# A gated feed-forward layer with quantised activations: the place of a sum, the fillers' budget, a bank's first write and the order of the tail

## The chip, the cores and the metric

The kernel runs on one core of a Trainium2 chip. The metric is the device time of one execution in microseconds (us), the median of three runs. TensorE is called PE here, VectorE DVE, ScalarE ACT, GpSimd POOL; SP is the engine that issues nearly all DMAs, in one queue that is taken strictly in order. Each engine also takes its own instructions in order: an instruction that waits holds up all that stand behind it on its engine.

## The reference

The input is x with four batches of 1024 tokens of 512 numbers, all in float32. For every batch the layer computes

```python
scale = cond @ norm_w.T + 1.0
h = x * (scale[:, None, :] * rsqrt(mean(x * x) + EPS))
u = h @ up_w.T                        # 512 -> 2 x 2048
val, gate = split(u, 2)
h = val * gelu(gate)                  # 2048 per token
hq = act_quant(h)                     # per token: round(h * 127/max|h|), and back
y = hq @ weight_quant(down_w).T + x   # weights -1, 0, 1 times a mean
```

(hq and the quantised weights are written there with a stop_gradient, which changes no value.) The maximum over a token's 2048 values has to be known before any of them can be rounded.

## The kernel before, in words

A batch has two halves of 512 tokens, and a half four tiles of 128 (a = 0 to 3). The 2048 hidden rows are 16 blocks j. For batch 1 and later the kernel works in *slots*, one for each block: `slot` (L581 on) issues the seven fast-multiplication products of the up projection of block g = 16 b + j (A, E, B banks of PSUM; each product is six 128x512 matmuls, L513). The products 3, 2 of the block before it are finished in the same slot. ACT applies the Gelu (L608, L624), DVE multiplies and writes the hidden values into H, a ring of 18 slots (L611, L630). In a slot there are places for other work: `early` at its start, `x`, `mid[0]`, `y`, `mid[1]`, `mid[2]`, `late`, `z`.

Batch b - 1 is quantised and multiplied by the down weights while batch b goes through its slots. DVE scales a piece of two blocks and one half (`quant_scale`, L705); it is rounded by one DVE instruction (`quant_round`, L709) or by two of ACT (`quant_up`, `quant_down`, L713, L717). The down product of token tile a of both halves is one `Pair`, done in slot j = 10 + a of batches 1 and 2 (`DOWN`), also as a fast multiplication, with sums instead of an eighth product. Its steps are:

- `sum1` (L760): the pair's first sum, on DVE, written into the H place of the next block, which is not yet in use as such. In slot 11 that place is still the source of a DMA transpose of token tile 0 of the next batch (L499).
- `sums` (L767 to L769): three more sums on DVE.
- `first`: B11 into bank k1, an ACT copy (L792), T1 into k3, which takes the first sum as its weights, B21 onto k1.
- `third`: T2, an ACT copy (L801), and DVE adds k3 to the rows of x (`onto`, L824).
- `fourth`: B22, T3, an ACT copy (L810), DVE L824 for k1.
- `fifth`: T4 onto k2, which needs that copy, DVE L824 for k2, and the two stores (L819).

The three banks k1, k2, k3 rotate through the PSUM tag "po". Before the first pair of all, `late` writes each of the three once with a matmul named po_set (L1307).

`next_pair` makes the pair of the next slot and issues its `sum1`. In the slot before the first pair it runs in `mid[0]` behind the weight sums (`d_sums`, L417: 2 x 1.2 us on DVE each); in the others in `early`, behind the running pair's `sums`.

The next batch's tokens are prepared in the same slots: ACT squares (L447), DVE L421 and POOL L422 make the factor, ACT (L459) and POOL (L460) scale, POOL adds (L468 to L471), ACT and DVE split into high and low parts (L492, L496), and SP's transpose brings them into place.

DVE's other work comes from a list, the `Filler`: maxima over pairs of blocks (L647, L649) and the pieces. At `x` and `z` of each slot it takes from the list what a budget allows: `left` is a slot's length less what is known to be in it, `cap` the part for `x`. The order on each engine is thus fixed when the program is made.

In the tail batch 3 has no slots after it. Pair 3 of batch 2 is done as plain products there (`down_mm`, L733, for both halves, and `down_end`, L742), next to pair 2 in the fast form (`old[2]`). Then come the two halves of batch 3: `half_steps` gives the scaling and rounding of their eight pieces, `token_turn` (L682) and `token_undo` (L688) send the maxima through DRAM and bring them back as a factor for each token (dq_end), which DVE inverts and scales (`bring_dq`, L691, L692). `down_end` multiplies by it, adds x and stores (L743).

```python
def early():
    if down:
        pair.first([po_bank(f"po_{b}_{a}_{n}") for n in range(3)])
        pair.sums()
        next_pair()
    d_sums(early_sums)
```

Of the kernel before, what the change touches and what calls it, by code (L numbers as in the profile page):

```python
# [18 lines left out]
P = 128  # L19
# [31 lines left out]
def glu_quant_kernel(  # L51
# [11 lines left out]
    B, S, D = x.shape  # L63
# [6 lines left out]
    NJ = FF // P  # L70
# [80 lines left out]
    def po_bank(name, shape=None):  # L151
        return bank("po", 3, shape, name)
# [1050 lines left out]
    for b in range(1, B):  # L1203
        dve, act = Filler(), Filler()
        gains(b)
        am = am_tile(b - 1)
        dq = state[b - 1] = sm.tile([P, 2 * NA], F32, name=f"dq_{b}", tag="dq")
        last_pair = NJ // 2 - 1
        for h in range(2):
            add_pair(  # L1210
                dve, act, b - 1, last_pair, h, (0, "xz"[h]),
                lambda now, h=h: token_max(b - 1, h, am),
            )
        for h in range(2):
            for cost, f in token_scale(h, am):
                dve.add((1, "x"), cost, lambda now, f=f: f())
        add_pieces(dve, act, b - 1, am, PIECES, (2, "x"))
        for i in range(NJ // 2 - 1):
            for h in range(2):
                add_pair(dve, act, b, i, h, (2 * i + 3, "x"))  # L1220
        steps = {}
        pairs = {}
        if b + 1 < B:
            sc = cond_load_scale(b + 1)
            bring = lambda b=b, sc=sc: cond_bring(b + 1, sc)
            steps[1, "z"] = [(bring, (0.4, 0))]
            p0 = b * NJ + 12
            plan = [
                (None, p0, ((6, "z"), (7, "x"), (7, "y"), (9, "y"), (10, "x"), (10, "z"))),
                (p0 + 4, None, ((9, "y"), (10, "x"), (10, "y"), (11, "y"), (12, "x"), (12, "x"))),  # L1230
                (None, None, ((10, "y"), (11, "x"), (11, "y"), (13, "x"), (13, "y"), (13, "z"))),
                (p0 + 2, p0 + 4, ((9, "z"), (12, "x"), (12, "y"), (14, "x"), (14, "y"), (14, "z"))),
            ]
            for a, (at, nx_at, places) in enumerate(plan):
                def make(a=a, at=at, nx_at=nx_at, b=b):
                    toks[a] = Tokens(b + 1, a, at, nx_at)
                    toks[a].load()
                fs = [
                    make,
                    lambda a=a: toks[a].norm(),  # L1240
                    lambda a=a, sc=sc: toks[a].scale(sc),
                    lambda a=a: toks[a].high(),
                    lambda a=a: toks[a].low(DVE),
                    lambda a=a: toks[a].turn(),
                ]
                costs = ((0, 0), (0, 1.6), (0, 1.5), (0, 2.1), (2.6, 0), (0, 0))
                for place, f, c in zip(places, fs, costs):
                    steps.setdefault(place, []).append((f, c))
        for j in range(NJ):
            g = b * NJ + j  # L1250
            down = b + 1 < B and j in DOWN
            if down:
                pair, a = pairs[j], DOWN[j]
                xrs = [down_load(b - 1, h, a) for h in range(2)]
            early_sums, late_sums = D_SUM_AT.get((b, j), ((), ()))
            left = SLOT_US + PAIR_US * down - OWN_US + 0.4
            left -= D_SUM_US * (len(early_sums) + len(late_sums))
            mine = {p: [sum(c[e] for _, c in steps.get((j, p), ())) for e in range(2)] for p in "xyz"}
            left -= sum(mine[p][0] for p in "xyz")
            act_left = {"x": 2.7, "y": 2.2 if down else 1.1, "z": 0}  # L1260

            def run(p):
                nonlocal left
                for f, _ in steps.get((j, p), ()):
                    f()
                if p == "x":
                    cap = min(left, 3.9 - mine["x"][0] - (0 if down else mine["y"][0]))
                    left -= cap - dve.run((j, p), cap)
                elif p == "z":
                    left = dve.run((j, p), left)  # L1270
                if p != "z":
                    act.run((j, p), act_left[p] - mine[p][1])

            def early():
                if down:
                    pair.first([po_bank(f"po_{b}_{a}_{n}") for n in range(3)])
                    pair.sums()
                    next_pair()
                d_sums(early_sums)

            def next_pair():
                if b + 1 < B and j + 1 in DOWN:
                    pairs[j + 1] = Pair(b - 1, DOWN[j + 1])
                    pairs[j + 1].sum1(h_slots(g + 1)[:, 0, 0])

            def more_sums():
                d_sums(late_sums)
                next_pair()

            mid = [nothing] * 3  # L1290
            if j + 1 == min(DOWN):
                mid[0] = more_sums
            if down:
                mid = [lambda: (pair.third(xrs, dq), d_sums(late_sums)), pair.fourth, lambda: (loads(), pair.fifth())]

            def loads():
                if NJ + 2 <= g + 2 < B * NJ:
                    s_load_x(g + 2)
                if NJ + 2 <= g + 1 < B * NJ:
                    s_load_y(g + 1)  # L1300


            def late():
                if b == 1 and j + 1 == min(DOWN):

                    for n in range(3):
                        PE.matmul(  # L1307
                            po_bank(f"po_set_{n}").rearrange("p (a t) -> p a t", t=P),
                            s_tile(g + 1)[:, 0, 0, :P], t_view(b)[:, :, 0, 0, 0, :],
                            start=True, stop=True,  # L1310
                        )

            if b + 1 == B and j in DOWN and DOWN[j] < 3:
                pairs[DOWN[j]] = Pair(b - 1, DOWN[j])
                places = old_places(DOWN[j])
                pairs[DOWN[j]].sum1(places[0])
                pairs[DOWN[j]].sums(*places[1:])
            if j == 4:
                token_turn(b - 1, am)
            if j == 5:  # L1320
                bring_dq = token_undo(b - 1, dq)
            if j == 6:
                bring_dq()
            if j == NJ - 1:
                get_ready()
            elif b == 1 and j == 0:
                get_ready()
            slot(g, lambda: run("x"), lambda: run("y"), lambda: run("z"), early, mid, late)
            if not down:
                loads()  # L1330
        assert not act.items and not dve.items, (b, dve.items, act.items)
# [59 lines left out]
    def half_steps(h):  # L1391
        for i in range(NJ // 2):
            yield lambda i=i: quant_scale(b, i, h, am)
            if i % 3 == 2:
                yield lambda i=i: quant_round(b, i, h)
            else:
                def rounds(i=i):
                    quant_up(b, i, h)
                    quant_down(b, i, h)
                yield rounds  # L1400
# [24 lines left out]
    for f in work[2:7]:  # L1425
        f()
    down_mm(b - 1, 0, 3, pos[0], range(NJ // 2, NJ))
    down_mm(b - 1, 1, 3, pos[1], range(NJ))
    old[2].fifth()
    for f in work[7:11]:  # L1430
        f()
    for h in range(2):
# [2 lines left out]
        f()  # L1435
    work = [f for _, f in token_scale(1, am)] + [lambda: token_turn(b, am, 1, 2)]
    work += list(half_steps(1))
    for h in range(2):
        bring_dq = token_undo(b, dq, h, h + 1)
        if h == 0:  # L1440
            pos = [po_bank(f"po_end_0_{a}") for a in range(3)] + [bank("E", 2, name="po_end_0_3")]
        else:
            pos = [bank(t, 1 if t == "B" else 2, name=f"po_end_1_{n}") for n, t in enumerate("ABEA")]

        ys = [2] * (NA - 1) + [1 if h else 2]
        cut = NJ - 4
        for j in range(0, cut, 2):
            for a in range(NA):
                down_mm(b, h, a, pos[a][:, : HALF * ys[a]], (j, j + 1), 0, ys[a])
            for f in work[:4]:  # L1450
                f()
            del work[:4]
        for f in work:
            f()
        work = []
        bring_dq()
        for a in range(NA):
            c, xr = slice(0, HALF * ys[a]), XR[:, h * NA + a]
            down_mm(b, h, a, pos[a][:, c], range(cut, NJ), 0, ys[a])
            down_end(b, h, a, pos[a][:, c], xr[:, c], dq, c)  # L1460
# [30 lines left out]
```

## Time and profile before

| what | value |
|---|---|
| median of three runs | 749.37 us (748.68 to 750.09) |
| the profiled execution | 749.7 us, span 747.5 us |
| granted TensorE clock, mean | 0.997 |
| busy: DVE, ACT, POOL | 80%, 52%, 28% of the span |
| DMA, mean | 148 GB/s |
| chain that ended last, largest parts | PE 83%, no wait shown ("issue") 6%, DVE 4%, POOL 3% |

The profile is one execution. Its span goes from the first to the last instruction on the chip; the 2.2 us that the execution's own time is longer lie around it. "Busy" of PE uses modelled ends of matmuls, since they overlap in the array; starts are recorded. A row of the timeline has the start, the time, the engine, the line of the kernel, the operation, what it writes and reads, a count, and in brackets how long the engine had been idle before and what ended that. A row of the waits says which engine and line waited for which, how long in all, how often, and the longest. In the table by stages each engine has its busy time and, in brackets, its instructions; behind them are the granted clock, the busy share of the DMA engines and their rate.

### The profile page before, as it was taken

Reading aid. Unit: us, or ns where it says so; the run is one execution under the profiler, and the core shown is the slowest. Engines: PE = TensorE matmul, PEld = TensorE weight load, DVE = VectorE, ACT = ScalarE, POOL = GpSimd, SP = SyncE. Lnnn points to the kernel's source line nnn. Section 1 sums busy time; section 2 is a strip of 40 time slices with the busy share of each in tenths; the row PEclk is TensorE's granted clock in tenths of the full one; section 3 lists DMA queues with packets and bytes.
Section 4 is the critical chain, followed back from the end, with each engine's and each line's share of the span. In section 5 each row is a group of like instructions: output and inputs, shape, how many; then the busy total and the mean of one; then the engine's idle time right before and its main releaser. Section 6 shows DMA issues by size and latency. Waiting matters only on the chain.

```text
span 747.5 us, 10283 instructions
## 1 busy us (share of the span) xinstructions
PE 733.9 (98%) x3766; PEld 371.5 (50%) x3766; DVE 596.0 (80%) x868; ACT 387.2 (52%) x649; POOL 210.8 (28%) x221
## 2 busy tenths in 40 slices
PE   7999999999999999999999999999999999999997
PEld 3545545544444445665444444666444444445743
DVE  6968699897889889697679897587678888755896
ACT  5757465565235675544434666453433666332364
POOL 1499487899010030552010030343020000000100
PEclk9999999999999999999999999999999999999999
DMA  6289629765523434756922425646933332222343
GB/s 237 70 294 202 238 98 247 210 174 170 159 88 107 139 110 156 177 142 195 214 99 99 127 99 184 164 138 156 220 110 112 109 106 99 100 98 85 123 146 112
DMA packets 90141, 110.47 MB, mean 148 GB/s; under 512 B 57190, under 2 KB 58087, under 8 KB 90092
## 3 DMA queue, kind: packets, MB, share of 16 engines
q1 hardware_dynamic: 89802, 109.50, 48.9%
q8 instruction: 29, 0.48, 0.3%
q10 hardware_dynamic: 290, 0.33, 0.1%
q14 instruction: 20, 0.16, 0.1%
HBM read 74.66 MB, written 23.09 MB: 131 GB/s over the span
## 4 chain that ended last, share of the span: by engine, by line
PE 83%; issue 6%; DVE 4%; POOL 3%; ACT 1%; DMA 1%; SPq 0%; DVEq 0%; POOLq 0%; ACTq 0%
PE A L513 29%; PE E L513 15%; PE pg L528 11%; PE pv L528 11%; PE B L513 7%; PE po L784 6%; PE pw L296 2%; DVE H L705 2%; PE po L733 1%; DMA H<-in_x_dram 1%; POOL xn L460 1%; PE ptx L874 1%; POOL H L460 1%; DVE R L742 0%; PE po_B L784 0%
## 5 line engine op out<-in xcount | busy, mean ns | idle before, releaser
L513 PEld LDWEIGHTS <-SXY 128*128 128x128 f16 x2016 | 197.3, 98 | 232.2 <-issue 0.6
L513 PE MATMUL A<-R,SXY 128*128 128x512 f16 x1152 | 266.3, 379 | 0.0
L513 PE MATMUL E<-R,SXY 128*128 128x512 f16 x576 | 140.0, 379 | 0.0
L611 DVE SCALAR_TENSOR_TENSOR H<-A,sg,t 128x512 f32<-128x512 f32 x48 | 36.0, 750 | 65.6 <-PE A L513 65.4
L663 POOL PARTITION_ALL_REDUCE am<-R x8 | 14.3, 1793 | 227.9 <-DVE R L649 227.9
L705 DVE TENSOR_TENSOR H<-H,am 128x1024 f32<-128x1024 f32 x64 | 76.2, 1217 | 0.0
L624 ACT ACTIVATE t<-t,sg 128x512 f32<-128x512 f32 x48 | 34.6, 721 | 75.0 <-DVE t L621 75.0
L513 PE MATMUL B<-R,SXY 128*128 128x512 f16 x288 | 70.0, 379 | 0.0
L647 DVE TENSOR_REDUCE gm<-H 128x512 f32<-128x1024 f32 x56 | 69.0, 1231 | 1.0
L422 POOL TENSOR_TENSOR rs<-ssq,neghalf 128x2 f32<-128x2 f32 (+1 forms) x13 | 9.9, 765 | 195.1 <-DVE ssq L421 194.9
L528 PE MATMUL pv<-R 128*128 128x512 f16 x246 | 61.6, 379 | 0.0
L784 PE MATMUL po<-wd,R 128*128 128x256 fp8e4 (+1 forms) x448 | 57.0, 275 | 2.6 <-ACT po L810 1.7
L528 PEld LDWEIGHTS <-SXY 128*128 128x128 f16 x378 | 36.9, 98 | 42.4
L528 PE MATMUL pg<-R,SXY 128*128 128x512 f16 x252 | 57.8, 379 | 0.0
L528 PEld LDWEIGHTS <-R 128*128 128x128 f16 x366 | 35.8, 98 | 41.8
L784 PEld LDWEIGHTS <-R 128*128 128x128 bf16 (+1 forms) x480 | 46.9, 98 | 16.3 <-issue 3.3
L608 ACT ACTIVATE t<-B,sg 128x512 f32<-128x512 f32 x48 | 33.0, 687 | 36.2 <-PE B L513 36.2
L713 ACT ACTIVATE H<-H 128x1024 f32<-128x1024 f32 x39 | 40.9, 1049 | 15.0 <-DVE H L705 14.9
L591 ACT COPY t<-A 128x512 f32<-128x512 f32 x48 | 27.9, 582 | 39.8 <-PE A L513 39.5
L599 ACT COPY B<-A 128x512 f32<-128x512 f32 x48 | 27.4, 572 | 37.9 <-PE A L513 37.3
L603 ACT COPY v<-E 128x512 f32<-128x512 f32 x48 | 28.1, 585 | 31.1 <-PE E L513 27.8
L630 DVE SCALAR_TENSOR_TENSOR H<-v,sg,t 128x512 f32<-128x512 f32 x48 | 37.7, 784 | 7.6 <-ACT t L624 7.6
(190 smaller groups left out, 1038.0 us busy)
## 6 DMA issues: line engine op xcount, KB each, us to landing
SXY<-s_dram SPq DMA_DIRECT2D x48, 640.0 KB, 4.0
SXY<-s_dram SPq DMA_DIRECT2D x48, 256.0 KB, 4.3
s_dram<-SXY SPq DMA_DIRECT2D x11, 896.0 KB, 4.3
H<-in_L_cond_up_w_dram SPq DMA_DIRECT2D x32, 256.0 KB, 5.1
xr<-in_x_dram SPq DMA_DIRECT2D x19, 256.0 KB, 2.9
out_dram<-xr SPq DMA_DIRECT2D x19, 256.0 KB, 4.0
s_dram<-R SPq DMA_DIRECT2D x5, 896.0 KB, 5.8
H<-in_x_dram SPq DMA_DIRECT2D x8, 512.0 KB, 4.6
```

The lines of the kernel that those rows point to most:

```text
L513: PE.matmul(o, s[:, w, k, :], tv[:, :, c, l, k, :], start=start and n == 0, stop=stop and n == len(TERMS) - 1, skip_group_check=True,)
L528: PE.matmul(ps, a[k // 2][:, w, k % 2, :], XP[:, l, k, h * TOK : (h + 1) * TOK], start=n == 0, stop=n == len(terms) - 1,)
L591: ACT.copy(cur["t2"], cur["A"])
L603: ACT.copy(cur["v"], cur["E"])
L608: ACT.activation(cur["t1"], pb, AF.Gelu, scale=gain(g, 1))
L611: DVE.scalar_tensor_tensor(h_half(g - 1, 0), prev["A"], gain(g - 1, 0), prev["t1"], ALU.mult, ALU.mult)
L624: ACT.activation(prev["t2"], prev["t2"], AF.Gelu, scale=gain(g - 1, 1))
L630: DVE.scalar_tensor_tensor(h_half(g - 1, 1), prev["v"], gain(g - 1, 0), prev["t2"], ALU.mult, ALU.mult)
L647: DVE.tensor_reduce(gm[0], v, AX.X, ALU.max, apply_absolute_value=True)
L705: DVE.tensor_tensor(v, v, r.to_broadcast([P, 2, TOK]), ALU.mult)
L713: ACT.activation(v, v, AF.Copy, bias=MAGIC)
L784: PE.matmul(po, w[:, j], m, start=start and j == 0, stop=stop and j == n - 1, skip_group_check=True,)
```

## The change

It has five parts.

1. `next_pair` goes from `early` into `mid[1]`, behind `fourth`: the next pair's first sum stands on DVE behind the L824 of k1 and in front of L627, the L824 of k2 and L630. The slot before the first pair keeps it in `mid[0]`.
2. The fillers' budget counts, in `left` and in the cap for `x`, the late weight sums, and 0.7 for the first sum in the slot before the first pair. With it, in slot 9 of batch 1 one reduce (L647) no longer stands in front of the weight sums, but comes in slot 11; in slot 9 of batch 2 one reduce goes from in front of the first sum to behind L630; one or two L649 in slots 11 and 12 of batch 1 move by some places. Behind slot 12 the order is the old one in both batches.
3. `late` writes one of the three banks with po_set, not all.
4. In the tail, half 1's pieces 1, 4 and 7 are rounded by DVE, before it were 2 and 5; the rest by ACT. The last of `old[2]`, T4, stands between the halves of the last plain product and not behind it.
5. The load of the second half's factors is issued in front of the first half's four stores on SP, and not behind them.

```diff
-            left -= D_SUM_US * (len(early_sums) + len(late_sums))
+            more = D_SUM_US * len(late_sums) + 0.7 * (j + 1 == min(DOWN) and b + 1 < B)
+            left -= D_SUM_US * len(early_sums) + more
...
-                    cap = min(left, 3.9 - mine["x"][0] - (0 if down else mine["y"][0]))
+                    cap = min(left, 3.9 - mine["x"][0] - (0 if down else mine["y"][0] + more))
...
                     pair.sums()
-                    next_pair()
                 d_sums(early_sums)
...
-                mid = [lambda: (pair.third(xrs, dq), d_sums(late_sums)), pair.fourth, lambda: (loads(), pair.fifth())]
+                mid = [lambda: (pair.third(xrs, dq), d_sums(late_sums)), lambda: (pair.fourth(), next_pair()), lambda: (loads(), pair.fifth())]
...
-                    for n in range(3):
-                        PE.matmul(
-                            po_bank(f"po_set_{n}").rearrange("p (a t) -> p a t", t=P),
-                            s_tile(g + 1)[:, 0, 0, :P], t_view(b)[:, :, 0, 0, 0, :],
-                            start=True, stop=True,
-                        )
+                    banks = [po_bank(f"po_set_{n}") for n in range(3)]
+                    PE.matmul(
+                        banks[1].rearrange("p (a t) -> p a t", t=P),
+                        s_tile(g + 1)[:, 0, 0, :P], t_view(b)[:, :, 0, 0, 0, :],
+                        start=True, stop=True,
+                    )
...
-            if i % 3 == 2:
+            if i in ((1, 4, 7) if h else (2, 5)):
                 yield lambda i=i: quant_round(b, i, h)
...
-    down_mm(b - 1, 1, 3, pos[1], range(NJ))
+    down_mm(b - 1, 1, 3, pos[1], range(NJ // 2))
     old[2].fifth()
+    down_mm(b - 1, 1, 3, pos[1], range(NJ // 2, NJ))
...
+    bring_dq = [token_undo(b, dq, 0, 1)]
     for h in range(2):
-        bring_dq = token_undo(b, dq, h, h + 1)
...
-        bring_dq()
+        if h == 0:
+            bring_dq.append(token_undo(b, dq, 1, 2))
+        bring_dq[h]()
```

## The prediction

> **What bounds the kernel now.** I read the page first, then the waits of PE, then PE by stages, then the timeline around each wait. A first look:
>
> ```profile
> PE 733.9 (98%) x3766; PEld 371.5 (50%) x3766; DVE 596.0 (80%) x868; ACT 387.2 (52%) x649; POOL 210.8 (28%) x221
> L784 PE MATMUL po<-wd,R 128*128 128x256 fp8e4 (+1 forms) x448 | 57.0, 275 | 2.6 <-ACT po L810 1.7
> ```
>
> PE is busy all the time but 13.6 us of 747.5. So only two things can move the time: matmuls that go, and PE's holes. By stages:
>
> ```profile
> 198.20:320.00 121.80, 120.53 (x616) 60.05 (x614) 103.57 (x134) 66.62 (x107) 23.66 (x19) 1.00 0.43 129
> 320.00:350.00 30.00, 29.29 (x186) 17.99 (x185) 25.53 (x37) 11.98 (x25) 11.21 (x13) 1.00 0.51 147
> 350.00:451.00 101.00, 101.00 (x473) 46.05 (x471) 82.23 (x107) 53.19 (x80) 10.55 (x9) 1.00 0.45 132
> 451.00:525.00 74.00, 73.28 (x447) 43.46 (x445) 54.83 (x81) 36.44 (x70) 21.80 (x22) 1.00 0.58 171
> 525.00:680.00 155.00, 155.00 (x719) 70.25 (x718) 115.04 (x150) 71.94 (x107) 3.94 (x3) 1.00 0.39 119
> ```
>
> (First numbers: length, PE busy.) Between 350 and 451, and 525 and 680, PE has no hole at the full clock: what is won earlier is handed on whole. The holes lie where the change works: slots 10 to 13 of batches 1 and 2 (286 to 337 and 459 to 515), and the tail after 713. The timeline of PE has them:
>
> ```profile
> 289.24 1.03 PE L784 MATMUL po<-wd,R 128*128 128x256 fp8e4 x8 [0.28 <-ACT po L792]
> 318.20 1.47 PE L784 MATMUL po<-wd,R 128*128 128x256 fp8e4 x11 [0.96 <-ACT po L810]
> 334.36 0.81 PE L784 MATMUL po<-wd,R 128*128 128x256 fp8e4 x6 [0.71 <-ACT po L810]
> 461.96 1.03 PE L784 MATMUL po<-wd,R 128*128 128x256 fp8e4 x8 [0.47 <-ACT po L792]
> ```
>
> The brackets use modelled ends; I count from starts, at 0.216 us a 512-wide matmul (12 take 2.59 in the chain of waits) and 0.109 a 256-wide one (16 take 1.75). T1's eight start at 287.92 and should end at 288.79: hole 0.45. The six of product 6 start at 315.78, end 317.08: hole 1.12. Likewise from 332.19: 0.87; from 460.45: 0.64. At 489.80 sixteen matmuls (one 512 wide) end at 491.65 and T1 starts at 492.22: 0.57, a fifth hole. Sum 3.65 us.
>
> Why are the ACT copies late? DVE and ACT at the second hole:
>
> ```profile
> 313.94 0.69 DVE L760 TENSOR_TENSOR H<-R 128x1024 bf16<-128x1024 bf16 x1 [6.46 <-DMA R<-H]
> 315.21 0.16 DVE L421 TENSOR_SCALAR ssq<-ssq 128x2 f32<-128x2 f32 x1
> 316.55 1.34 ACT L459 ACTIVATE xn<-xn,rs 128x512 f32<-128x512 f32 x2 [1.47 <-POOL rs L422]
> 317.79 0.36 ACT L810 COPY po<-po 128x256 f32<-128x256 f32 x1
> ```
>
> DVE stood 6.46 us in front of the next pair's first sum (L760), whose place in H the DMA transpose is still reading. Behind it queue L611, L421 (POOL's and then ACT's scaling wait for that), so ACT's copy L810, and PE's T4. Batch 2 has the same wait (5.2 us).
>
> The tail, again from the timeline:
>
> ```profile
> 713.43 0.75 DVE L824 SCALAR_TENSOR_TENSOR SXY<-po,dq,SXY 128x512 f32<-128x512 f32 x1 [1.66 <-PE po L784]
> 727.95 1.69 PE L733 MATMUL po_end<-wd,R 128*128 128x512 fp8e4 x8 [0.61 <-ACT R L717]
> 729.99 12.72 PE L733 MATMUL po_end<-wd,R 128*128 128x512 fp8e4 x72 [0.35 <-ACT R L717]
> 738.67 0.42 SPq L688 DMA_DIRECT2D dq_end<-am_dram  x1
> 740.98 0.18 DVE L691 RECIPROCAL dq_end<-dq_end 128x4 f32<-128x4 f32 x1 [2.75 <-DMA dq_end<-am_dram]
> 741.53 2.85 DVE L742 SCALAR_TENSOR_TENSOR R<-po_end,dq_end,R 128x512 f32<-128x512 f32 x5
> ```
>
> PE's last matmul ends at about 742.55, but the kernel waits for DVE, whose last sum ends at 744.38: the factor load (L688) sat behind four stores on SP's queue. After that only a store and the closing follow (3.14 us, unchanged).
>
> **The change, part by part** (times in the clock of before; each part then moves what follows).
>
> *Two po_set matmuls go:* 2 x 0.216 = 0.43 us on PE, wholly on the path (286.29 to 286.94 has no hole). A load wait of the first stays with the one left.
>
> *Fillers that count the sums:* in slot 9 of batch 1 the reduce L647 (1.23) leaves its place before the weight sums (L417), L760 and L621. L621 then ends at 286.9, ACT's Gelu L624 at 287.7, the copy L792 at 288.07, before PE wants B21 (288.36, po_set counted): hole 0.45 gone. In batch 2's slot 9 another L647 (1.24) goes behind: L792 ends at about 460.8, B21 is wanted at 461.32: 0.64 gone. The moved reduces land in slots 9 to 11, where DVE now has the 6.5 and 5.2 us it stood still; nothing that PE wants soon is behind them.
>
> *The sum L760 after `fourth`.* Slot 11: L611 can run at 310.65 (product 3 ends), L421 at 311.5 (ACT's accumulations), POOL's power by 312.4. ACT reaches L459 at 315.1 after its casts and L810 at 316.5; T4 is wanted at 317.08: 1.12 gone. Slot 12: L611 loses the L760 in front and follows PE; L421 at 328.75, L459 from 329.6, L810 at 331.1, T4 wanted at 332.35: 0.87 gone. Batch 2, slot 11: the L824 that free the banks come earlier; 0.57 gone. Behind the moved L760 now queue L627, L824 of k2, L630: half a microsecond later each. The out stores wait for that L824, on SP the transpose of token tile 0 waits behind them, and the next x rows behind that (7.28 us of issue): from 311.8 to 312.4, landing (3.2) near 316.2. DVE's first L824 of slot 11 waits for them; PE's next T1 still follows later.
>
> *What L760 costs at its new place:* T1 of the next slot needs it. Without disturbance it ends, against T1's wish, at 303.2 against 303.64 (slot 10), 318.55 against 318.93 (slot 11), 332.0 against 334.2; in batch 2 all margins are over 1 us. Here a rule speaks against the change. The row: L760 took 0.674 to 0.693 us in all eleven, none of them beside POOL work. At its new place stands POOL's L460. The Trainium skill (SBUF — State Buffer, Who interferes with whom) says that a DVE instruction with two SBUF inputs and a GpSimd one that reads SBUF take the shared ports in turn, the later one blocked for the other's whole instruction. The nearest row agrees:
>
> ```profile
> 336.76 1.18 POOL L469 TENSOR_TENSOR H<-H 128x256 f32<-128x256 f32 x1
> 337.28 1.21 DVE L767 TENSOR_TENSOR R<-R 128x1024 bf16<-128x1024 bf16 x1
> ```
>
> L767 takes 0.69 alone. By L760's own rows the sum is 0; by L767's (+0.53) T1 waits 0.1 and 0.15; by the rule, blocked by all of an L460 (1.27), T1 waits 0.8 in slot 10's successor, 0.2 after slot 11, 0.2 in batch 2: 1.2. I take 0.6, and keep 0 to 1.2.
>
> Slots: 0.43 + 3.65 - 0.6 = 3.5 us (2.9 to 4.1).
>
> *Tail, T4 between the halves of the last plain product.* PE's work is the same, T4 comes 8 x 0.216 = 1.73 earlier (its copy L810 was ready at 708.8). DVE's wait of 1.66 goes, and DVE runs without a gap from there to 735, so all of half 1's scaling is 1.7 earlier. Its first product no longer waits: from 727.95 to 727.18, 0.77 won.
>
> *Rounding of pieces 1, 4, 7 by DVE:* DVE gets one L709 more (0.65 with its spacing), ACT loses an L713 and an L717 (2.1). PE's second and third waits go (0.53 and 0.20): piece 1 is rounded at 725.8, wanted at 728.7; ACT's last piece ends at 735.2, wanted at 736.4. PE then ends at 742.55 - 1.5 = 741.05.
>
> *Factors in front of the stores:* the load goes out when its row has landed (about 725); behind it only stores that wait until 735. DVE then: first half's sums 734.5 to 737.2, two factor steps, second half's sums as PE delivers. The last starts 0.3 after PE's end and takes 0.48: 741.85, against 744.38. Tail: 2.5 us. If only the load worked: PE ends at 742.55, DVE at 743.3: 1.1. If only the other two: DVE is 1.0 earlier (1.7 less one L709) and so is the load: 1.0. So 1.0 to 2.6.
>
> **Sum.** 3.5 + 2.5 = 6.0. The profiled execution took 749.7 (span 747.5), the median of the three runs is 749.37: 743.7 and 743.4.
>
> **Rivals.**
> 1. *The port decides.* L760 waits for POOL at every pair, the stores and x rows shift, T1 waits about 2 us more in all: 745.4. For it: two margins under 0.5. Against: four over 1.
> 2. *The tail gives half:* DVE's order or the load works alone, 1.0: 744.9. Against it: DVE shows no other wait after 713.
> 3. *The change doesn't do what it says:* T4's copy stays late because of ACT's own casts (L492, 313.21 to 315.1), not L760; 1.12 + 0.87 remain: 745.4. Against: ACT idled 1.47 behind them for POOL.
> 4. *Slower:* the moved sum itself becomes the bound. If it comes 4 us late, behind both L460 and POOL's four sums, T1 waits 3.5, 3.6, 1.8 in batch 1 and 1.7, 2.6, 2.0 in batch 2: 15 us, 749.4 - 6.6 + 15.2 = 758. It decides from a lateness of about 2.8 us in each of the six slots. Against: DVE's longest stretch by the port in these rows is one POOL instruction.
>
> **How the numbers follow.** Forecast (742.4 to 744.4): 0.62. Rival 1: 0.15, rival 2: 0.10, rival 3: 0.06; more than counted, below 742.4: 0.02; no change by another cause: 0.03; rival 4: 0.02. From 742.4 to 745.8 hold the forecast and most of rivals 1 to 3, together 0.86. A measurement of this kernel tells about 0.2% (1.5 us) from nothing: faster 0.95, same 0.03, slower 0.02.
>
> **What would show it.** Right: in PE's waits L810 and L792 are gone or under 0.3 us each; DVE's wait L760 <- DMA is gone; the L742 of the second half follow PE without a wait for dq_end; PE has no hole between 713 and its end. Wrong: a wait of PE for DVE's L760 at T1, L760 rows of over 1.2 us, a DVE wait for x rows at L824 in slot 11, or PE holes elsewhere in 350 to 680.

## The result, and the profile after

| | before | after |
|---|---|---|
| median of the runs, one chip | 749.73 us (748.68 to 751.47, 4 runs) | 742.84 us (741.79 to 743.98, 4 runs) |
| the profiled execution, span | 749.7 us, 747.5 us | 742.87 us, 740.7 us |

The ratio is 0.9906, with a 95% interval of 0.9882 to 0.9930: faster by 0.94%. The forecast was 743.4 us. The first lines of the page, after:

```profile
PE 731.6 (99%) x3764; PEld 370.6 (50%) x3764; DVE 602.2 (81%) x869; ACT 385.3 (52%) x647; POOL 212.8 (29%) x221
...
PE 98%; DMA 1%; DVE 0%; ACT 0%; issue 0%; SPq 0%; DVEq 0%
...
L784 PE MATMUL po<-wd,R 128*128 128x256 fp8e4 (+1 forms) x448 | 56.8, 275 | 0.0
```

Two matmuls are gone, and PE is idle for 9.1 us of the span where it was 13.6. This group of L784 has lost its idle time (2.6 before, of it 1.7 behind ACT's copy L810). The chain of waits now runs through PE for 98% of the span. The waits of PE from 60 us to the end (what it waited for, us in all, times, longest), before and then after:

```profile
PE po L784 <- ACT po L810: 1.7, 2, 1.0
PE po_end L733 <- ACT R L717: 1.0, 2, 0.6
PE po L784 <- ACT po L792: 0.8, 2, 0.5
```

```profile
PE po L784 <- DVE H L760: 0.6, 1, 0.6
```

All the waits for ACT's copies and rounding are gone; one for the moved sum L760 is new. By stages:

```profile
320.00:350.00 30.00, 30.00 (x186) 17.87 (x184) 26.33 (x37) 12.74 (x25) 11.04 (x11) 1.00 0.58 160
...
451.00:525.00 74.00, 74.00 (x453) 44.18 (x452) 57.52 (x80) 37.51 (x72) 23.61 (x22) 1.00 0.62 176
```

These two had 0.71 and 0.72 us of PE's idle time and have none. The one hole left where the change works is in slot 10 of batch 1 (the timeline of DVE, POOL and PE):

```profile
298.74 3.79 POOL L460 TENSOR_TENSOR H<-H,sc 128x512 f32<-128x512 f32 x2 [0.83 <-ACT H L459]
...
301.34 1.73 DVE L760 TENSOR_TENSOR H<-R 128x1024 bf16<-128x1024 bf16 x1
...
303.13 1.05 PE L784 MATMUL po<-wd,H 128*128 128x256 fp8e4 x8 [0.59 <-DVE H L760]
```

The sum that took 0.69 us before takes 1.73 here; its first 1.19 us lie beside POOL's scaling (to 302.53), and 0.54 behind it. PE's T1, which takes the sum as its weights, starts 0.75 late (302.27 to 303.13 between starts, less 0.109). In slot 11 the wait is gone that the prediction began with:

```profile
310.27 0.75 DVE L611 SCALAR_TENSOR_TENSOR H<-A,sg,t 128x512 f32<-128x512 f32 x1 [2.22 <-PE A L513]
310.97 0.17 DVE L421 TENSOR_SCALAR ssq<-ssq 128x2 f32<-128x2 f32 x1
...
316.24 0.86 DVE L760 TENSOR_TENSOR H<-R 128x1024 bf16<-128x1024 bf16 x1
```

L421, on which POOL's power and ACT's scaling wait, starts at 310.97 and not at 315.21. The tail:

```profile
709.48 27.83 PE L733 MATMUL po_end<-wd,R 128*128 128x512 fp8e4 x144
...
720.17 0.37 SPq L688 DMA_DIRECT2D dq_end<-am_dram  x1
...
733.47 0.17 DVE L691 RECIPROCAL dq_end<-dq_end 128x4 f32<-128x4 f32 x1
...
737.35 0.48 DVE L742 SCALAR_TENSOR_TENSOR R<-po_end,dq_end,R 128x256 f32<-128x256 f32 x1 [0.89 <-PE po_end L733]
```

The 144 matmuls from 709.48 on run in one piece; before, they had three waits for the rounding, and one of 0.21 for a bank (at 714.23). The factors' load goes out at 720.17 and not at 738.67. L691 runs in its turn, where it had waited 2.75, and the last L742 waits for PE alone.

**Where the time went, by starts of instructions.** The first L528 is PE's first product of batch 0's up projection, the last L513 the end of the slots. (us)

| stretch | before | after | difference | forecast |
|---|---|---|---|---|
| start to the first L528 | 22.35 | 21.95 | -0.40 | 0 |
| from there to the last L513 ("slots") | 674.85 | 671.57 | -3.28 | -3.5 |
| from there to PE's last matmul ("tail of PE") | 45.25 | 43.52 | -1.73 | -1.5 |
| from there to the end of DVE's last sum | 1.94 | 0.80 | -1.14 | -1.0 |
| closing | 3.14 | 2.87 | -0.27 | 0 |
| span | 747.52 | 740.71 | -6.81 | -6.0 |

The tail of PE repeats to a few hundredths of a microsecond from kernel to kernel where an edit doesn't touch it (it is 43.52 in the changed kernel and eight of those below, 45.25 in the one before and three of those below). So do the slots of the changed kernel (671.57 to 671.60 with e3, e5 and e6, whose edits lie behind them); those of the kernel before are 674.85, but 674.66 in e11, whose edit doesn't touch them either, so a difference of 0.2 to that kernel proves nothing. The start-up doesn't repeat, over a range of 2.4 us, and it moves the whole time. So the experiments are judged by these stretches, with the ratios of whole times beside them.

### The profile page after: what moved, and what is told of

Read it like the earlier page. It is cut to its first block, busy times and chain, and to the rows that moved or that the text cites. A ratio compares the mean times of both kernels' runs of the same rounds, so it can differ in the third digit from the quotient of the medians.

```text
span 740.7 us, 10277 instructions
## 1 busy us (share of the span) xinstructions
PE 731.6 (99%) x3764; PEld 370.6 (50%) x3764; DVE 602.2 (81%) x869; ACT 385.3 (52%) x647; POOL 212.8 (29%) x221
## 4 chain that ended last, share of the span: by engine, by line
PE 98%; DMA 1%; DVE 0%; ACT 0%; issue 0%; SPq 0%; DVEq 0%
PE A L513 34%; PE E L513 17%; PE pg L528 11%; PE pv L528 11%; PE B L513 8%; PE po L784 8%; PE po_end L733 4%; PE pw L296 2%; PE po L733 1%; DMA H<-in_x_dram 1%; PE ptx L874 0%; PE po_B L784 0%; PE pv L571 0%; PE pg L571 0%; PE po_A L784 0%; DVE H L760 0%
## 5 line engine op out<-in xcount | busy, mean ns | idle before, releaser
L513 PEld LDWEIGHTS <-SXY 128*128 128x128 f16 x2016 | 197.3, 98 | 232.2 <-issue 0.6
L513 PE MATMUL A<-R,SXY 128*128 128x512 f16 x1152 | 266.3, 379 | 0.0
L513 PE MATMUL E<-R,SXY 128*128 128x512 f16 x576 | 140.0, 379 | 0.1
L611 DVE SCALAR_TENSOR_TENSOR H<-A,sg,t 128x512 f32<-128x512 f32 x48 | 36.0, 750 | 71.9 <-PE A L513 71.7
L513 PE MATMUL B<-R,SXY 128*128 128x512 f16 x288 | 70.0, 379 | 0.0
L647 DVE TENSOR_REDUCE gm<-H 128x512 f32<-128x1024 f32 x56 | 69.0, 1233 | 1.0
L422 POOL TENSOR_TENSOR rs<-ssq,neghalf 128x2 f32<-128x2 f32 (+1 forms) x13 | 10.0, 766 | 186.2 <-DVE ssq L421 186.1
L528 PE MATMUL pv<-R 128*128 128x512 f16 x246 | 61.6, 379 | 0.0
L528 PEld LDWEIGHTS <-SXY 128*128 128x128 f16 x378 | 37.0, 98 | 42.3
L528 PE MATMUL pg<-R,SXY 128*128 128x512 f16 x252 | 57.8, 379 | 0.0
L784 PE MATMUL po<-wd,R 128*128 128x256 fp8e4 (+1 forms) x448 | 56.8, 275 | 0.0
L528 PEld LDWEIGHTS <-R 128*128 128x128 f16 x366 | 35.8, 98 | 41.8
L784 PEld LDWEIGHTS <-R 128*128 128x128 bf16 (+1 forms) x480 | 46.9, 98 | 12.8
L649 DVE TENSOR_TENSOR R<-R,gm 128x512 f32<-128x512 f32 x56 | 43.1, 770 | 1.4
```

The source lines that it names most:

```text
L513: PE.matmul(o, s[:, w, k, :], tv[:, :, c, l, k, :], start=start and n == 0, stop=stop and n == len(TERMS) - 1, skip_group_check=True,)
L528: PE.matmul(ps, a[k // 2][:, w, k % 2, :], XP[:, l, k, h * TOK : (h + 1) * TOK], start=n == 0, stop=n == len(terms) - 1,)
L611: DVE.scalar_tensor_tensor(h_half(g - 1, 0), prev["A"], gain(g - 1, 0), prev["t1"], ALU.mult, ALU.mult)
L647: DVE.tensor_reduce(gm[0], v, AX.X, ALU.max, apply_absolute_value=True)
L649: return [largest, lambda: DVE.tensor_tensor(m, m, gm[0], ALU.max)]
L784: PE.matmul(po, w[:, j], m, start=start and j == 0, stop=stop and j == n - 1, skip_group_check=True,)
```

## The experiments

**Theory.** DVE's wait for the transpose in front of L760 made the copies late that T4 needs; the moved sum pays for it where it runs beside POOL; in the tail T4, the rounding and the load each remove a wait of their own. **Rivals.** The copies are late through ACT's own casts. The new hole in slot 10 comes of a bank that isn't free, and not of POOL. The gain lies in one part, and the others are along for the ride. Diffs are against the changed kernel, except where "on before" is said.

### The sum put back (e1)

```diff
                     pair.sums()
+                    next_pair()
...
-                mid = [..., lambda: (pair.fourth(), next_pair()), ...]
+                mid = [..., pair.fourth, ...]
```

> The changed kernel with the next pair's first sum back in early. My theory (DVE stands in front of that sum and holds up the token factors, so ACT's copy before T4 is late): the holes of PE at T4 in slots 11 and 12 of batch 1 (1.12 and 0.87 us) and the 0.57 in batch 2 come back, the new hole of 0.75 at T1 of slot 11 goes: 1.8 us longer, about 744.6. Rival (ACT's own casts make the copy late): no holes come back, and the time is 0.7 us shorter, about 742.1.

Slots 673.39, which is 1.82 more than after; ratio to the kernel before 0.9949 (0.9931 to 0.9968). DVE again waits 6.2 us for the transpose in front of L760. PE's rows:

```profile
315.62 1.03 PE L784 MATMUL po<-wd,R 128*128 128x256 fp8e4 x8 [0.33 <-ACT po L810]
...
332.55 1.69 PE L784 MATMUL po<-wd,R 128*128 128x256 fp8e4 x13 [0.58 <-ACT po L810]
```

The size is the theory's, net of slot 10's hole, which is gone here. Its make-up is not: with the other parts in place T4 waits 0.49 in slot 11 (by starts) where it waited 1.12, and the matmul at 317.12 waits 0.63 for DVE's L824. Behind it T1 waits another 0.26; slot 12 has 0.74, and batch 2 has 0.41 for L824. Together 2.53, less the 0.75 that left: 1.78 of the 1.82.

### Another place to write, the order of before (e2, on before)

Slot 11's sum goes to another H place, one that no transpose reads.

```diff
-                    pairs[j + 1].sum1(h_slots(g + 1)[:, 0, 0])
+                    pairs[j + 1].sum1(h_slots(g + (4 if j == 11 else 1))[:, 0, 0])
```

> The kernel before, with the first sum of slot 11 written to another place in H, which no transpose reads. My theory says that the wait for the transpose makes the hole at T4 in slot 11: DVE's waits of 6.5 and 5.2 us go, and the holes of 1.12 and 0.57 with them, but 0.87 in slot 12 stays, because there the sum's own 0.69 us stands in front: 1.7 us shorter than before, about 748.0. Rival (slot 12's hole is what slot 11 left over): all three go, 2.6 us shorter, about 747.2. If ACT's casts make the copy late: nothing changes.

Slots 672.33, 2.52 less than before: the rival's 2.6, not my 1.7. Ratio 0.9960 (0.9945 to 0.9976). DVE's wait for the transpose made the holes of 1.12, 0.87 and 0.57: all three are gone, though the sum stands where it stood. In slot 12:

```profile
324.48 0.68 DVE L760 TENSOR_TENSOR H<-R 128x1024 bf16<-128x1024 bf16 x1
...
327.81 0.16 DVE L421 TENSOR_SCALAR ssq<-ssq 128x2 f32<-128x2 f32 x1
...
330.18 0.36 ACT L810 COPY po<-po 128x256 f32<-128x256 f32 x1
```

T4 starts at 331.22, 0.7 us after that copy's end and without a hole. In the kernel before DVE had no gap from 313.94 on, so what it lost in slot 11 was still missing in slot 12. I had put that hole down to the 0.69 us of the sum in front of L611 in slot 12.

### Only slot 11's sum moved (e9)

```diff
                     pair.sums()
+                    if j != 11:
+                        next_pair()
...
-                mid = [..., lambda: (pair.fourth(), next_pair()), ...]
+                mid = [..., lambda: (pair.fourth(), next_pair() if j == 11 else None), ...]
```

> The changed kernel, with the sums of slots 10 and 12 back in early and only that of slot 11 after fourth. If the hole of 0.87 us in slot 12 was what slot 11 had left over (as the kernel with the other place showed), it stays away and the hole at T1 goes too: the stretch from the first L528 to the last L513 is 670.8 us against 671.57 of the changed kernel, about 742.1. If the sum's own place in slot 12 made it, 0.87 comes back: 671.7.

Slots 672.00: neither 670.8 nor 671.7. Slot 10's hole of 0.75 is gone, but slot 12 has a hole of 1.22 that the changed kernel doesn't have. The timeline of DVE, POOL and PE:

```profile
315.21 1.62 DVE L760 TENSOR_TENSOR H<-R 128x1024 bf16<-128x1024 bf16 x1
...
328.58 0.16 DVE L421 TENSOR_SCALAR ssq<-ssq 128x2 f32<-128x2 f32 x1
...
328.83 1.07 POOL L422 TENSOR_TENSOR rs<-ssq,neghalf 128x2 f32<-128x2 f32 x1 [8.36 <-DVE ssq L421]
...
331.58 2.01 PE L784 MATMUL po<-wd,R 128*128 128x256 fp8e4 x16 [1.06 <-ACT po L810]
```

So what e2 suggested, "slot 12's hole was only left over from the wait", doesn't hold in general. Here DVE had no wait for a transpose. From L611 of slot 11 to L421 of slot 12 it runs without a gap both here and in the changed kernel, and that takes 19.81 us here (308.77 to 328.58) and 18.54 there (310.27 to 328.81): 1.27 more. Two items make most of it, counted from start to start: slot 12's sum stands in front of L611 (0.60), and slot 11's sum takes 0.76 longer, since it meets nearly a whole L460 of POOL's and not the end of one. (The reduce that the new budget puts into slot 11 is in both.) The copy L810 is 1.26 later against PE for it. The changed kernel had 0.09 to spare there, from the copy's end at 331.76 to T4 at 331.85; e2 had 0.7. My reading is that slot 12 is late when DVE carries too much from slot 11 on, whatever it is: 6.5 us of waiting, or longer work of its own. Which of the two items alone would be enough was not tried.

### Is slot 10's hole POOL's? (e4 and e8)

e4 puts slot 10's sum back into `early`, where POOL stands still. e8 leaves the sum and moves POOL's scaling of that tile from `y` to `z` of the slot.

```diff
 # e4
+                    if j == 10:
+                        next_pair()
...
-                mid = [..., lambda: (pair.fourth(), next_pair()), ...]
+                mid = [..., lambda: (pair.fourth(), None if j == 10 else next_pair()), ...]
 # e8
-                (p0 + 4, None, ((9, "y"), (10, "x"), (10, "y"), ...
+                (p0 + 4, None, ((9, "y"), (10, "x"), (10, "z"), ...
```

> The changed kernel, with the first sum of slot 10 alone back in early, where POOL does nothing. Theory of the shared ports: that sum takes 0.69 instead of 1.73 us, the hole of 0.75 us at T1 of slot 11 goes, nothing else comes back: 742.1, that is 0.75 us shorter than the changed kernel. Rival (T1 waits for the bank that the L824 in front of the sum sets free): the hole stays at 0.6 or more and the time is that of the changed kernel, 742.8.

> The changed kernel, with the scaling of token tile 1 (ACT L459, POOL L460) moved from y to z of slot 10, so that the sum keeps its place and POOL is not beside it. Theory of the shared ports: the sum takes 0.69, the hole at T1 goes, 0.75 us shorter, 742.1, unless the later scaling makes a new wait in slot 11. Rival (the bank): the sum's length makes no difference, hole 0.6 or more, 742.8.

Slots 670.80 and 670.82, 0.77 and 0.75 less than after; the hole is gone in both. In e8 the sum stands where it stands in the changed kernel:

```profile
300.82 0.68 DVE L760 TENSOR_TENSOR H<-R 128x1024 bf16<-128x1024 bf16 x1
...
301.69 2.95 POOL L460 TENSOR_TENSOR H<-H,sc 128x512 f32<-128x512 f32 x2 [4.31 <-ACT H L459]
...
301.86 1.04 PE L784 MATMUL po<-wd,H 128*128 128x256 fp8e4 x8
```

0.68 and not 1.73, and T1 without a wait. The same banks are in use, so the rival of the bank falls. These two are the shortest kernels by the stretches: PE has no hole over 0.21 us from the first L528 to its end. By the whole time they aren't told apart from the changed kernel: ratios 0.9918 (0.9897 to 0.9939) and 0.9905 (0.9887 to 0.9922), medians 742.73 and 742.02 us.

### The budget, the banks (e7, e10, e12)

e7 has the old two lines of the budget; e10 writes all three banks in the changed kernel; e12 writes one bank on before, and nothing else.

```diff
 # e7
-            left -= D_SUM_US * len(early_sums) + more
+            left -= D_SUM_US * (len(early_sums) + len(late_sums))
...
-                    cap = min(left, 3.9 - mine["x"][0] - (0 if down else mine["y"][0] + more))
+                    cap = min(left, 3.9 - mine["x"][0] - (0 if down else mine["y"][0]))
 # e10 (e12 does the reverse, on before)
-                    PE.matmul(
-                        banks[1].rearrange("p (a t) -> p a t", t=P),
...
+                    for v in banks:
+                        PE.matmul(
+                            v.rearrange("p (a t) -> p a t", t=P),
```

> The changed kernel, with the fillers' budget as before. My theory: the reduces are back in front of the sums in slot 9, and PE's holes of 0.45 us (batch 1) and 0.62 us (batch 2) at B21 of slot 10 come back: 1.1 us longer, 743.9. Rival (the later sum alone leaves DVE room enough): no holes there, no change, 742.8.

> The changed kernel, with po_set written to all three banks again. With no hole behind it each matmul is on the path: the stretch from the first L528 to the last L513 is 0.43 us longer, 672.0, about 743.3. Rival (they lie under the wait for ACT's copy at B21): no change, 671.57.

> The kernel before, with po_set written to one bank and nothing else. The prediction counted 0.43 us on the path. Theory after the runs so far: B21 waits for ACT's copy there, so PE comes to that wait 0.43 us earlier and stands that much longer: the hole grows from 0.45 to 0.75 or more, and the stretch from the first L528 to the last L513 stays within 0.15 us of 674.85. If the matmuls count: 674.42.

e7: slots 673.07, 1.50 more than after, where 1.1 was expected; ratio 0.9950 (0.9933 to 0.9966). e10: slots 671.98, 0.41 more, as expected; ratio 0.9919 (0.9901 to 0.9936). e12: slots 674.57, 0.28 less than before, where at most 0.15 was expected; ratio 0.9996 (0.9984 to 1.0009). The three belong together. PE's rows in e12:

```profile
288.69 1.05 PE L784 MATMUL po<-wd,H 128*128 128x256 fp8e4 x8
290.32 1.03 PE L784 MATMUL po<-wd,R 128*128 128x256 fp8e4 x8 [0.58 <-ACT po L792]
```

PE arrives 0.43 earlier, but neither the sum that T1 needs nor the copy that B21 needs is earlier. By starts T1 (288.69) waits 0.13 for L760, which it didn't before, and B21 (290.32) waits 0.74 for L792, where it waited 0.45: 0.42 of the 0.43 are waited away in slot 10. e7 has the same 0.13 and 0.74, and 0.64 in batch 2, which is its whole 1.50. The 0.28 that e12 is shorter comes later: 0.2 at T4 in slot 11 (0.91 for 1.12) and 0.1 in batch 2. It can't be put down to the edit, for e11 has the same 0.2 less at that T4 without it. With the budget counted the copy is early, and the two matmuls count in full (e10).

### The tail: T4, the rounding, the load (e5, e6, e3, e11)

```diff
 # e5
-    down_mm(b - 1, 1, 3, pos[1], range(NJ // 2))
+    down_mm(b - 1, 1, 3, pos[1], range(NJ))
     old[2].fifth()
-    down_mm(b - 1, 1, 3, pos[1], range(NJ // 2, NJ))
 # e6
-            if i in ((1, 4, 7) if h else (2, 5)):
+            if i % 3 == 2:
 # e3 (e11 does the reverse, on before)
-    bring_dq = [token_undo(b, dq, 0, 1)]
...
+        bring_dq = token_undo(b, dq, h, h + 1)
...
-        if h == 0:
-            bring_dq.append(token_undo(b, dq, 1, 2))
-        bring_dq[h]()
+        bring_dq()
```

> The changed kernel, with T4 back behind the whole last plain product. DVE waits 1.7 us for T4 again, the scaling of half 1 comes 1.7 us later, PE waits 0.77 us for its first piece, the later waits stay away since DVE rounds pieces 1, 4 and 7: 0.8 us longer, 743.6. Rival (the rounding alone keeps PE fed): no change, 742.8.

> The changed kernel, with ACT rounding six pieces of half 1 and DVE two, as before. If the two edits of the tail's order add up, as the prediction counted them: PE's waits of 0.53 and 0.20 us come back, 0.7 us longer, 743.5. Rival, worked out from the changed kernel's trace: with T4 early ACT's pieces come 1.7 us earlier and each is in time (piece 1 by 0.5, the last by 0.4 us): no wait, and no change, 742.8.

> The changed kernel, with the load of the second half's factors back behind the first half's stores. My theory: PE ends as in the changed kernel, but DVE waits again some 2.3 us for the factors; its last sum ends about 1.9 us later: 744.7. Rival (the load was covered, the order of the tail did it all): no change, 742.8.

> The kernel before, with the second half's factors loaded in front of the stores and nothing else. PE ends as before; DVE no longer waits for the factors and its last sum follows PE's last matmul as in the changed kernel, that is 0.80 us behind its start and not 1.94: 1.1 us shorter than before, about 748.3.

e5: the tail of PE is 44.94, 1.42 more than after, where 0.8 was expected; ratio 0.9954 (0.9937 to 0.9971). Its first long wait:

```profile
725.65 4.71 PE L733 MATMUL po_end<-wd,R 128*128 128x512 fp8e4 x24 [0.61 <-ACT R L717]
```

By starts this is the 0.77 that was forecast for T4. A second wait for L717, at 730.61, takes 0.41, though it was to stay away. A third of 0.21 stands at 711.92 (and stood at 714.23 before): the matmuls there wait for the L824 behind T4. e6: the tail of PE is 43.52, as after; ratio 0.9930 (0.9912 to 0.9948). With T4 early the old rounding costs nothing at all, so T4 alone is worth the whole 1.73. With T4 late the new rounding is worth 0.31 (45.25 less 44.94).

e3: the tail of PE is as after, and DVE's last sum ends 2.72 behind PE's last matmul, not 0.80; ratio 0.9944 (0.9931 to 0.9957). DVE's row in e3:

```profile
735.46 0.18 DVE L691 RECIPROCAL dq_end<-dq_end 128x4 f32<-128x4 f32 x1 [2.81 <-DMA dq_end<-am_dram]
```

e11, the load alone on before: 1.94 becomes 0.79, 1.15 won where 1.1 was worked out; ratio 0.9979 (0.9967 to 0.9991). The 1.94 itself varies: it is 2.22 in e2 and 2.15 in e12, whose tails are those of before. In e2 the load took 2.56 us to land, and 2.28 in the kernel before.

The closing, too, follows the load. It is 2.86 or 2.87 in every kernel that has the load in front of the stores, e11 among them, and 3.14 or 3.15 in every one that has it behind them (before, e2, e3, e12). So the 0.27 belongs to the fifth part; by what way the closing gets shorter is not shown.

## Why the prediction was right, step by step

- **PE's holes as the price list.** Right. The slots gave 3.28 where 3.5 was forecast, the tail 3.1 with the closing where 2.5 was. 743.4 lies 0.6 us from the median. The -0.40 of the start is no part of any step, it is luck (below). The -0.27 of the closing belongs to the load, and the prediction had put it at nothing ("unchanged").
- **The wait for the transpose.** Right, and e2 shows it to be the cause of all three holes that the moved sum was to remove. Wrong was the working for slot 12, "L611 loses the L760 in front": e2 loses that hole with L760 still in front. (In e9 the sum in front does cost PE time there, together with a longer sum in slot 11.)
- **What the sum costs at its new place.** Right in the mechanism; the size was in part luck. The 0.6 was taken between 0.25, by the nearest row (L767, +0.53), and 1.2, by the Trainium skill's rule (SBUF — State Buffer, Who interferes with whom) with the sum blocked for a whole instruction of POOL's. That 1.2 doesn't come out of its own figures: a block of 1.27 against the margin after slot 11 (318.55 to 318.93) makes T1 wait 0.9 there and not 0.2, and 1.9 in all. Measured was 0.75, all of it after slot 10, where the row gave 0.1 and the rule 0.8. The trace agrees with the rule at all six places: an L460 of POOL's is under way when the sum starts, and the sum ends 0.55 behind the end of that L460 (it took 1.73, 0.86 and 1.25 us in batch 1, 1.28, 0.86 and 1.27 in batch 2). So the sum is held up by the rest of the instruction under way, between 0.2 and 1.05 over its length alone, and only slot 10 had too little margin for that. e4 and e8 show that POOL is the cause there. Two of the prediction's signs of being wrong did appear, a wait of PE for L760 at T1 and L760 rows over 1.2 us: this term was too small by 0.15, and nothing else followed from it.
- **The fillers' 0.45 and 0.64.** Right as holes. As worth it is 1.50 (e7), since po_set's 0.43, which the prediction counted as "wholly on the path", is won only with it (e10, e12).
- **The x rows behind the transpose.** The forecast shift didn't come. On each kernel's own clock the transpose was issued 0.4 later (304.80), but held SP for 5.22 us and not 7.28, so the x rows were issued at 310.12 and not at 311.80, and no L824 waited for them.
- **T4 and the rounding.** The sum, 1.5, was right (1.73), the shares were not. Forecast 0.77 for T4 and 0.73 for the rounding; measured 1.42 for T4 and nothing for the rounding behind it (e5, e6). The term that was mis-sized is T4's: all of half 1's scaling is 1.7 us earlier with it, which by itself covers the second and third wait (e6); and the bank's 0.21 wasn't seen.
- **The load.** Right: 1.1 forecast for it alone, 1.15 measured (e11), and 0.28 of the closing besides.

Rival 1 (the port at every pair) was right in its mechanism, all six sums got longer beside POOL, and fell at its size, 0.75 and not 2. Rival 2, and with it the theory of one part that does it all, falls: the sum (e1, 1.82), the budget (e7, 1.50), T4 (e5, 1.42) and the load (e3, 1.92) all pay. Rival 3 (ACT's casts) falls with e1 and e2. Rival 4 needed a lateness of 2.8 us at each pair; the worst was 1.05.

## What to carry to other kernels

Read PE's holes as a price list, but not as a sum of independent prices: what is won in front of a wait whose other side doesn't move is waited away (0.42 of 0.43 at the next two waits in e12), and two edits that remove one wait are paid once (e5, e6). When an instruction is late, look for where its engine last had a gap: everything from there on is carried along, so a wait of 6.5 us in one slot is a hole in the next one too. Before a sum of two tensors like this one is moved on DVE, look at what POOL does at the new place, and count the rest of the POOL instruction under way there, at worst a whole one, against the margin.

## What was not expected of the hardware

The start-up differs from one profiled execution to the next, and no part of the change reaches there. The windows from 7 to 14 us, before and then after (the clock is the last column but two):

```profile
7.00:14.00 7.00, 4.83 (x27) 3.73 (x28) 3.71 (x17) 3.82 (x10) 2.28 (x3) 0.85 0.90 337
```

```profile
7.00:14.00 7.00, 4.37 (x29) 3.12 (x29) 3.74 (x18) 4.01 (x10) 1.85 (x3) 1.00 0.92 341
```

In the seven experiments with a granted clock of 1.00 there (e1 to e4, e7 to e9) the first L528 starts at 21.0 to 21.4 us; in the five with 0.83 to 0.91 (e5, e6, e10 to e12) at 23.0 to 23.4, and in the kernel before, with 0.85, at 22.35. The changed kernel, with 1.00, started at 21.95, so the clock isn't all of it, and that the clock is the cause is not shown.

A small instruction of POOL's also got longer beside DVE: L422 on 128x2 elements, 0.70 us at 298.47 in the kernel before, took 1.07 in e9 (328.83) beside a DVE L649 that began 0.2 us earlier, and 1.07 in the kernel before at 315.45, again 0.2 us behind the start of an L649.
